# Convolution, windowed attention and a contractive recurrence on one core: QKV as a stage of its own, the image with its borders in DRAM, evenly spaced recurrence streams with a sixth of W z on TensorE

## The chip, the cores and the metric

The kernel runs on one core of a Trainium2 chip. The metric is device time in microseconds (us), as the median of several runs. One execution was also recorded by the hardware profiler; all views of the profile are of that execution. Engine names: PE is TensorE (PEld its weight loads), DVE is VectorE, ACT is ScalarE, POOL is GpSimd, SP is SyncE, which issues most of the DMAs.

## What is computed

The input is 32 images of 128 channels and 64 x 64 pixels, all float32. Cut to what matters:

```python
x = x + conv3x3(groupnorm(x), sum_k coeff[b, k] * kernels[k])     # its own kernel for each image
t = tokens(x)                                                     # (32, 4096, 128)
u = layernorm(t)
att = windowed_attention(u @ w_down.T)       # width 16, 4 heads of 4, windows of 144, step 72
t = t + layernorm(u + sigmoid(gate) * (att @ w_up.T))             # times gamma, plus beta
z = layernorm(t) @ W.T                                            # batch norm over all images and tokens
y[s] = sigmoid(scale * z[s] + shift + y[s-1] @ V.T)               # 4096 steps
out = t + y
```

The batch norm needs the mean and variance of z over all images, so the recurrence can begin only when the last image is through the rest.

## The kernel before, in words

**The image stage** (function images, with its clock). Channels lie on the 128 partitions and the 4096 pixels of an image on the free axis. The work on one image b is cut into Python generators:

- load(b) fetches the image into one of two frames xs of 66 x 66 (the image with a border of one pixel), takes its group norm, and mixes the four kernels into wb on DVE, with eight loads kx from DRAM.
- conv(b) transforms strips of the frame (ut, on POOL and DVE), multiplies them by wb (48 products of 512 columns for one image, PE nm<-ut,wb) and adds the results to the frame on DVE (xs<-xs,nm).
- project(b) writes the frame's inside to x_d in DRAM by four DMAs of quarters, takes squares and means for the layer norm (PE nm<-xs,avg and nm<-place,avg), sends reciprocal deviations through DRAM (r_d) and gets them back spread over all partitions (place<-r_d), normalizes into zt, projects to width 16 (PE sc<-zt,wd), transposes (DVE gt), and makes queries, keys and values (PE sc<-gt,wqB, wkB and sc<-wvB). All this is one generator. Queries and keys have one buffer, so its last part waits until attend(b-1) is through.
- attend(b) does 14 sets of two half-steps each. A half-step is four score products (PE sc<-qe,ks), one exponential of 128 x 1152 (ACT ex<-sc), and eight weighted sums of the half-step before (PE av<-ex,VE); every second half-step has four more sums (av<-ext,VT) and every fourth has four more scores (sc<-qs,kt). The score tile sc fills four banks of PSUM and has one buffer, so the next scores wait for the exponential.
- divide(b, 0) and divide(b, 1) divide by the softmax sums: the sums go out by DMA (cd<-av), a reciprocal, back by DMA (av<-cd), are spread by PE (sc<-av,spr), and the result goes through the output projection (sc<-av,wc) into zt.
- tail(b) does the second and third layer norm, reading the image back from x_d (place<-x_d), writes the token stream to the output, multiplies by W (PE nm<-zt,fWc) and writes z to z_d.

Engines execute in the order in which instructions are written. That order comes from a planner at the end of images: each generator yields which engine it wants next and which tiles it needs; class Clock keeps estimated times of every engine, tile and DMA; the loop takes the step that can start first and, among those that can start when PE comes free, the one that stands first in a list sorted by a due time, b plus a constant of the stage. Convolutions sort last, so they fill what the others leave.

**The recurrence** (by_runs). V contracts, so the 4096 steps of an image are cut into 128 runs of 32, each warmed up by 20 steps of the run before; one step handles the 128 runs of two images at once (256 columns). The 16 groups of two images go through four streams, group g in stream g mod 4. One step is: PE product v<-yw,fVT, DVE v<-zr,scl,v (adds scale times z, read with a stride of 32 elements), ACT sigmoid into yw, and, in the 32 real steps, a POOL copy over z in place. After its 52 steps a group is added to the output by two accumulating DMAs that POOL issues, and only then may SP load group g+6 into the same one of six buffers zr. The streams take turns, one step each in a round; stream j begins 8 j rounds after stream 0.

The lines that matter in what follows: L173 is the line of the planner's wrapper, through which all instructions of the image stage go, so the rows of that stage are told apart by their tiles. L1597 loads z, L1617, L1620, L1621, L1622 are the warm-up steps, L1626, L1627, L1630, L1631 the real steps, L1634 the output.

Of the kernel before, what the change touches and what calls it, by code (L numbers as in the profile page):

```python
# [8 lines left out]
F32 = mybir.dt.float32  # L9
# [31 lines left out]
class Clock:  # L41
# [79 lines left out]
    def cost(self, eng, op, out, ins):  # L121
        n = max(self.width(a) for a in (out, *ins))
        if eng == "PE":
            n = self.width(ins[1])
            k, m = int(ins[0].ap[0][1]), self.width(ins[0])
            full = k == P and m == P
            c = n / 600 + 0.04 if full else n / 2400 + (0.06 if m == P else 0.025)
            c += 0.09 * (full != self.full)
            self.full = full
            return c, c  # L130
        if eng == "SP":
            run = min(int(a.ap[-1][1]) for a in (out, *ins))
            return 0.8, 2.5 + (1.2e-5 if run >= 512 else 4e-5) * n * int(out.ap[0][1])
        if eng == "ACT":
            c = 0.17 + 0.00084 * n
        elif eng == "DVE":
            c = 0.18 + 0.00106 * n
            if op == "reciprocal":
                c = 0.1 + 0.0067 * n
        else:  # L140
            c = 0.5 + 0.0013 * n
        return c, c
# [46 lines left out]
def hybrid_kernel(  # L189
# [35 lines left out]
    r_d = dram.tile([NB, 3, 2, T], F32, name="r_d")  # L225
    x_d = dram.tile([NB, P, T], F32, name="x_d")
    z_d = dram.tile([NB, P, T], F32, name="z_d")
# [108 lines left out]


    QT, NPL, NF, NZ = T // 4, 5, 2, 3

    def images(nc):  # L340
# [6 lines left out]
        with ExitStack() as pa:  # L347

            frm = pa.enter_context(tc.tile_pool(name="frm", bufs=1))
            xs = [frm.tile([P, H + 2, W + 2], F32, name=f"xs{i}") for i in range(NF)]  # L350

# [171 lines left out]

            places = [kept([P, 4, UNIT], f"place{i}") for i in range(NPL)]
            spare = list(places)

            def spread(jobs):

                todo, got = list(jobs), []
                while todo or got:  # L530
                    if todo and len(got) < 3 and spare:
                        yield "SP", None, (todo[0][0],), (spare[0],)
                        if spare:
                            w = spare.pop(0).rearrange("p r t -> p (r t)")
                            nc.sync.dma_start(w, todo[0][0])
                            got.append((w, *todo.pop(0)))
                    elif got:
                        w, _, aps, use = got[0]
                        yield "DVE", None, (w,) + aps
                        use(w)  # L540
                        got.pop(0)
                        spare.append(w.rearrange("p (r t) -> p r t", r=4))
                    else:
                        yield

            def place(eng, aps):
# [6 lines left out]
                return spare.pop(0)  # L553

            def deviations(src, b, k, mean):

                dims = "p (c r y) w -> p r c y w" if k == 0 else "p (c r t) -> p r c t"
                parts = src.rearrange(dims, c=4, r=4)
                for r in range(4):
                    sq = yield from place("ACT", (src,))  # L560
                    nc.scalar.activation(
# [15 lines left out]
                    for c in range(4):  # L577
# [6 lines left out]
                        )  # L584
                    spare.append(sq)
                rs = yield from place("ACT", (ps,))
                var = ps[:, 0:UNIT]
# [12 lines left out]
                for c in range(4):  # L600
# [3 lines left out]
                    )  # L604
                spare.append(rs)

# [139 lines left out]
            def project(b):  # L746
# [4 lines left out]
                yield "SP", None, (rows(xt, 0, H),)  # L751
                for i in range(4):
                    nc.sync.dma_start(lines(x_d[b, :, quarter(i)]), rows(xt, 16 * i, 16))
                yield from deviations(rows(xt, 0, H), b, 0, True)
                while (b and ("proj", b - 1) not in done) or (b >= NZ and ("tail", b - NZ) not in done):
                    yield
# [3 lines left out]
                def normed(i, k):  # L760
                    z = zt[:, quarter(i)]
                    src = r_d[b, 0, 1 - k, quarter(i)].partition_broadcast(P)
                    if k == 0:
                        xi = rows(xt, 16 * i, 16)
                        return src, (xi,), lambda w: nc.vector.tensor_mul(lines(z), xi, lines(w))
                    return src, (z,), lambda w: nc.vector.tensor_sub(z, z, w)

                yield from spread(normed(i, k) for i in range(4) for k in range(2))
                done["frame", b] = True
                yield "PE", "sc", (zt[:, 0:T],)  # L770

# [35 lines left out]
                )  # L807
                while b and ("sets", b - 1) not in done:
                    yield
                yield "PE", "sc", (gt,)  # L810
                qs = one.tile([P, GT], F32, name="qs")
# [236 lines left out]
            def tail(b):  # L1048
# [5 lines left out]
                def second(i, k):  # L1054
                    z = zt[:, quarter(i)]
                    if k == 0:
                        return (
                            r_d[b, 1, 1, quarter(i)].partition_broadcast(P),
                            (z,),
                            lambda w: nc.vector.scalar_tensor_tensor(z, z, gam, w, ALU.mult, ALU.mult),  # L1060
                        )
                    return (
                        x_d[b, :, quarter(i)],
                        (z,),
                        lambda w: nc.vector.scalar_tensor_tensor(z, z, bet, w, ALU.add, ALU.add),
                    )
# [10 lines left out]
                def third(i):  # L1077
                    z = zt[:, quarter(i)]

                    def use(w):  # L1080
                        nc.vector.tensor_mul(z, z, w)
                        for j in range(2):
                            nc.vector.bn_stats(st[:, 2 * i + j, :], z[:, BLK * j : BLK * (j + 1)])

                    return r_d[b, 2, 1, quarter(i)].partition_broadcast(P), (z,), use
# [22 lines left out]
            for b in range(NB):  # L1108
                for stage, g in enumerate(
                    (tail(b), divide(b, 0), divide(b, 1), attend(b), project(b), load(b), conv(b))  # L1110
                ):
                    jobs.append([stage == 6, b + (0.4, -0.3, -0.3, 0.45, -0.65, -2.2, 0)[stage], b, g, None])
            while jobs:
# [17 lines left out]
    def images_by_shift():  # L1131

        with ExitStack() as pa:
            keep = pa.enter_context(tc.tile_pool(name="keep", bufs=1))
            NG5 = NH * (HD + 1)
            kT = keep.tile([P, NK, 9, P], F32, name="kT")
            nc.sync.dma_start(kT, conv_k.rearrange("m k i j l -> m k (i j) l"))

            avg = keep.tile([P, 2 * P], F32, name="avg")
            nc.vector.memset(avg, 0.0)  # L1140
            nc.vector.memset(avg[:, P : P + 1], 1.0 / P)

            row = keep.tile([P, NBLK, P], F32, name="row")
            nc.vector.tensor_copy(
# [71 lines left out]
            nc.gpsimd.memset(gx, 0.0)  # L1216
            mx = keep.tile([HALF, NWG, 2, P], F32, name="mx")
            nc.gpsimd.memset(mx, 0.0)
# [337 lines left out]
    with arm.Else():  # L1556
        images_by_shift()


# [20 lines left out]
    def by_runs():  # L1580
# [3 lines left out]
        with ExitStack() as pb:  # L1584
            zp = pb.enter_context(tc.tile_pool(name="zp", bufs=NSTR + 2))
            hp = pb.enter_context(tc.tile_pool(name="hp", bufs=1))
            p_v = pb.enter_context(tc.tile_pool(name="p_v", bufs=2, space=bass.MemoryType.PSUM))
            pb.enter_context(tc.manual_schedule())

# [3 lines left out]
            def load(g):  # L1593
                if g < NG:
                    zs[g] = zp.tile([P, NI, NRUN, RUN], F32, name="zr")
                    for i in range(NI):
                        nc.sync.dma_start(  # L1597
# [3 lines left out]
            for g in range(NSTR + 2):  # L1601
                load(g)

            def stream(j):
# [4 lines left out]
                for g in range(j, NG, NSTR):  # L1609
# [4 lines left out]
                    for r in range(RUN - WARM, RUN):  # L1614
# [3 lines left out]
                        else:  # L1618
                            ps = p_v.tile([P, NI, NRUN], F32, name=f"v{j}")[:, :, 1:]
                            nc.tensor.matmul(ps, fVT, yw[1 - r % 2][:, :, 1:], start=True, stop=True)  # L1620
                            nc.vector.scalar_tensor_tensor(ps, z, scl, ps, ALU.mult, ALU.add)  # L1621
                            nc.scalar.activation(y, ps, AF.Sigmoid, bias=shf)  # L1622
                        yield
                    for r in range(RUN):
                        ps = p_v.tile([P, NI, NRUN], F32, name=f"v{j}")
                        nc.tensor.matmul(ps, fVT, yw[1 - r % 2], start=True, stop=True)  # L1626
                        nc.vector.scalar_tensor_tensor(  # L1627
                            ps, zt[:, :, :, r], scl, ps, ALU.mult, ALU.add
                        )
                        nc.scalar.activation(yw[r % 2], ps, AF.Sigmoid, bias=shf)  # L1630
# [12 lines left out]
            step = 0  # L1643
            lag = 8
            while live:
# [117 lines left out]
```

## Time and profile before

| | us |
|---|---|
| median of three runs (lowest, highest) | 5713.89 (5710.51, 5716.48) |
| the profiled execution | 5711.31 |
| its span, first to last instruction | 5709.5 |
| PE busy | 4745.7 |
| DVE busy | 3681.2 |
| ACT busy | 2390.4 |
| POOL busy | 1594.0 |
| first exponential of attention, last one starts | 227.3, 4983.0 |
| last instruction on z, first on the recurrence's statistics | 5064.4, 5068.5 |
| first step of the recurrence | 5082.9 |
| last PE product | about 5676 |
| granted PE clock, mean | 0.925 |

A row of the profile's groups gives line, engine, operation, tiles (out<-in), shapes, the number of instructions, then busy time and mean length in ns, then the idle time of the engine just before them and what ended it. A float32 product shows as two PE records. A row of the stage windows gives the stretch, its length, busy time of PE, PEld, DVE, ACT and POOL with the number of instructions, the granted PE clock, the DMA engines' share and GB/s.

### The profile page before, as it was taken

How to read it: one execution, taken by the hardware profiler on the slowest of the kernel's cores; microseconds unless marked ns; L12 is line 12 of the kernel's file. 1: busy time of each engine (PE TensorE's matmuls, PEld its weight loads, DVE VectorE, ACT ScalarE, POOL GpSimd, SP SyncE). 2: the span in 40 equal slices, each digit the busy share in tenths (PEclk: the TensorE clock that was granted, in tenths of full speed). 3: DMA queues.
4: the chain of work that ended last, by engine and by line, in shares of the span. 5: the costliest groups of instructions: out<-in, count | busy, mean ns of one | idle time of the engine just before them, and what ended most of it. 6: DMA issues, size and time to landing. Idle time of an engine off the chain costs nothing. (4 is left out here: it accounts for less than half of the span.)

```text
span 5709.5 us, 105290 instructions
## 1 busy us (share of the span) xinstructions
PE 4745.7 (83%) x43443; PEld 2330.2 (41%) x43443; DVE 3681.2 (64%) x5175; ACT 2390.4 (42%) x3564; POOL 1594.0 (28%) x1561
## 2 busy tenths in 40 slices
PE   2898988898898897988898888888889887648886
PEld 1444434444444443444444444444444444314443
DVE  4656666666676666666666666666666665348886
ACT  0243434334444444444444434434444444326664
POOL 1232213122322222222232222322232221105555
PEclk9999999999899899999999999999989989869987
DMA  4535454545454445454644445454544444265887
GB/s 106 142 98 156 139 173 117 176 130 157 132 157 138 148 134 169 128 158 135 197 130 146 141 145 164 139 155 143 167 148 149 140 147 139 77 251 148 237 238 144
DMA packets 716380, 861.92 MB, mean 151 GB/s; under 512 B 560992, under 2 KB 571504, under 8 KB 687216
## 3 DMA queue, kind: packets, MB, share of 16 engines
q1 hardware_dynamic: 707184, 787.93, 44.4%
q0 software_dynamic: 8704, 67.11, 5.7%
q8 instruction: 347, 5.69, 0.4%
q14 instruction: 145, 1.19, 0.1%
HBM read 573.00 MB, written 273.68 MB: 148 GB/s over the span
## 5 line engine op out<-in xcount | busy, mean ns | idle before, releaser
L173 ACT ACTIVATE ex<-sc 128x1152 f32<-128x1152 f32 x896 | 1012.0, 1129 | 1344.6 <-PE sc L173 1334.3
L173 PE MATMUL nm<-ut,wb 128*128 128x512 f32 x3072 | 1540.1, 628 | 19.2 <-DVE wb L173 13.0
L173 PE MATMUL sc<-qe,ks 32*128 32x288 f32 x7168 | 731.1, 478 | 332.9 <-ACT ext L173 123.2
L173 POOL TENSOR_TENSOR qe<-qs,mqk 128x576 f32<-128x576 f32 x448 | 607.2, 1360 | 1412.2 <-PE sc L173 1358.9
L173 POOL TENSOR_TENSOR ut<-xs 128x576 f32<-128x576 f32 x384 | 549.7, 1461 | 1002.7 <-PE nm L173 784.6
L173 PEld LDWEIGHTS nm<-ut,wb 128*128 128x128 f32 x3072 | 540.3, 193 | 641.7 <-issue 610.7
L173 PE MATMUL av<-ex,VE 128*32 128x144 f32 x14336 | 659.7, 304 | 70.8 <-DVE av L173 70.4
L173 PEld LDWEIGHTS sc<-qe,ks 32*128 32x128 f32 x7168 | 301.8, 193 | 830.2 <-issue 280.5
L173 DVE TENSOR_TENSOR xs<-xs,nm 128x512 f32<-128x512 f32 (+1 forms) x640 | 494.4, 791 | 220.4 <-PE nm L173 208.0
L173 PEld LDWEIGHTS av<-ex,VE 128*32 128x32 f32 x14336 | 374.5, 113 | 411.3 <-issue 259.1
L173 DVE TENSOR_TENSOR zt<-zt,place 128x1024 f32<-128x1024 f32 x256 | 340.0, 1328 | 132.8 <-DMA place<-r_d 97.4
L1631 POOL COPY zr<-yw 128x256 f32<-128x256 f32 x512 | 302.9, 702 | 381.4 <-ACT yw L1630 220.4
L173 ACT ACTIVATE place<-zt 128x1024 f32<-128x1024 f32 x256 | 263.1, 1052 | 207.6 <-DVE zt L173 202.0
L1626 PE MATMUL v<-yw,fVT 128*128 128x256 f32 x1024 | 320.1, 439 | 22.6 <-ACT yw L1630 22.1
L173 DVE SCALAR_TENSOR_TENSOR wb<-kx,co,wb 128x768 f32<-128x768 f32 x192 | 254.0, 1323 | 113.9 <-DMA kx<-k_d 111.9
L1627 DVE SCALAR_TENSOR_TENSOR v<-zr,scl,v 128x256 f32<-128x256 f32 x512 | 308.2, 682 | 28.5 <-PE v L1626 27.1
L173 DVE TENSOR_TENSOR place<-place 128x256 f32<-128x256 f32 x416 | 204.4, 492 | 181.3 <-ACT place L173 172.0
L1620 PE MATMUL v<-yw,fVT 128*128 128x254 f32 x608 | 205.5, 448 | 118.1 <-ACT yw L1617 102.7
L173 PE MATMUL nm<-place,avg 128*32 128x256 f32 x3072 | 238.8, 401 | 54.2 <-ACT place L173 54.0
L173 PE MATMUL nm<-zt,fWc 128*128 128x512 f32 x512 | 262.9, 652 | 17.7 <-DVE xs L173 13.1
L1630 ACT ACTIVATE yw<-v,shf 128x256 f32<-128x256 f32 x512 | 241.6, 473 | 82.0 <-DVE v L1627 41.2
L173 DVE SCALAR_TENSOR_TENSOR zt<-sc,gbc,zt 128x576 f32<-128x576 f32 (+1 forms) x192 | 175.4, 913 | 149.4 <-PE sc L173 149.0
(186 smaller groups left out, 5519.4 us busy)
## 6 DMA issues: line engine op xcount, KB each, us to landing
place<-r_d SPq DMA_DIRECT2D x512, 512.0 KB
kx<-k_d SPq DMA_DIRECT2D x256, 384.0 KB
xs<-in_x_dram SPq DMA_DIRECT2D x128, 512.0 KB
x_d<-xs SPq DMA_DIRECT2D x128, 512.0 KB
place<-x_d SPq DMA_DIRECT2D x128, 512.0 KB
out_dram<-zt SPq DMA_DIRECT2D x64, 1024.0 KB
z_d<-zt SPq DMA_DIRECT2D x64, 1024.0 KB
zr<-z_d SPq DMA_DIRECT2D x32, 2048.0 KB
```

The lines of the kernel that those rows point to most:

```text
L173: got = f(*args, **kw)
L1620: nc.tensor.matmul(ps, fVT, yw[1 - r % 2][:, :, 1:], start=True, stop=True)
L1626: nc.tensor.matmul(ps, fVT, yw[1 - r % 2], start=True, stop=True)
L1627: nc.vector.scalar_tensor_tensor(ps, zt[:, :, :, r], scl, ps, ALU.mult, ALU.add)
L1630: nc.scalar.activation(yw[r % 2], ps, AF.Sigmoid, bias=shf)
L1631: nc.gpsimd.tensor_copy(zt[:, :, :, r], yw[r % 2])
```

## The change

1. project(b) ends after the transpose (it leaves the tiles in done["gt", b]); a new generator feed(b) makes queries, keys and values. The next image's zt may be taken when ("gt", b-1) is done instead of ("proj", b-1). The due times of all stages change, and the planner's price of a DMA changes (0.6 instead of 0.8 us of SP, and the cheap rate from rows of 128 elements on, not 512).
2. The two frames become one constant tile, frames, that outlives the image stage. x_d has rows of 66 pixels, so the image goes out with its side borders by one DMA of 128 contiguous pieces (four DMAs of rows of 64 pixels before); place tiles grow from 1024 to 1056 elements, and the tail reads the inside of a bordered strip.
3. When the last image has left its frame, the z of group 0 is loaded into the frames, and groups 0, 6 and 12 of the recurrence use them; five buffers zr are left for the others.
4. Stream j begins 13 j rounds after stream 0 (52 / 4) instead of 8 j.
5. In the steps with (r + j) divisible by 6, PE multiplies z by a diagonal matrix of the scale (dg) and adds V y to it in PSUM, in place of DVE's instruction: 132 of the 816 steps.

```diff
-            return 0.8, 2.5 + (1.2e-5 if run >= 512 else 4e-5) * n * int(out.ap[0][1])
+            return 0.6, 2.5 + (1.2e-5 if run >= 128 else 4e-5) * n * int(out.ap[0][1])
...
-    x_d = dram.tile([NB, P, T], F32, name="x_d")
+    x_d = dram.tile([NB, P, H, W + 2], F32, name="x_d")
...
+    frames = const.tile([P, NI, (H + 2) * (W + 2)], F32, name="frames")
+    framed = frames[:, :, 0:T]
...
-                for i in range(4):
-                    nc.sync.dma_start(lines(x_d[b, :, quarter(i)]), rows(xt, 16 * i, 16))
+                nc.sync.dma_start(x_d[b], xt[:, 1 : H + 1])
                 yield from deviations(rows(xt, 0, H), b, 0, True)
-                while (b and ("proj", b - 1) not in done) or (b >= NZ and ("tail", b - NZ) not in done):
+                while (b and ("gt", b - 1) not in done) or (b >= NZ and ("tail", b - NZ) not in done):
                     yield
...
                 done["frame", b] = True
+                if b == NB - 1:
+
+                    yield "SP", None, ()
+                    for i in range(NI):
+                        nc.sync.dma_start(framed[:, i], z_d[i])
+                while b and ("proj", b - 1) not in done:
+                    yield
                 yield "PE", "sc", (zt[:, 0:T],)
...
-                while b and ("sets", b - 1) not in done:
+                done["gt", b] = zt, gt, gf, gtt
+
+            def feed(b):
+
+                while ("gt", b) not in done or (b and ("sets", b - 1) not in done):
                     yield
+                zt, gt, gf, gtt = done["gt", b]
                 yield "PE", "sc", (gt,)
...
-                    (tail(b), divide(b, 0), divide(b, 1), attend(b), project(b), load(b), conv(b))
+                    (tail(b), divide(b, 0), divide(b, 1), attend(b), project(b), load(b), conv(b), feed(b))
                 ):
-                    jobs.append([stage == 6, b + (0.4, -0.3, -0.3, 0.45, -0.65, -2.2, 0)[stage], b, g, None])
+                    jobs.append([stage == 6, b + (-0.05, -0.15, -0.15, 1.65, -1.4, -2.8, 0, -1.2)[stage], b, g, None])
...
-            zp = pb.enter_context(tc.tile_pool(name="zp", bufs=NSTR + 2))
+            zp = pb.enter_context(tc.tile_pool(name="zp", bufs=NSTR + 1))
...
+            dg = hp.tile([P, P], F32, name="dgs")
+            nc.vector.tensor_scalar_mul(dg, ident, scl)
...
+                    if g % (NSTR + 2):
+                        zs[g] = zp.tile([P, NI, NRUN, RUN], F32, name="zr")
+                    else:
+                        zs[g] = framed.rearrange("p i (c r) -> p i c r", r=RUN)
+                    for i in range(NI if g else 0):
...
+            def product(ps, z, y, n):
+
+                if n % 6:
+                    nc.tensor.matmul(ps, fVT, y, start=True, stop=True)
+                    nc.vector.scalar_tensor_tensor(ps, z, scl, ps, ALU.mult, ALU.add)
+                else:
+                    nc.tensor.matmul(ps, dg, z, start=True, stop=False)
+                    nc.tensor.matmul(ps, fVT, y, start=False, stop=True)
...
-            lag = 8
+            lag = (WARM + RUN) // NSTR
```

The second arm of the image stage (images_by_shift), which does not run here, takes some of its constants from the frames as well; nothing of it is in the profile.

## The prediction

> **What bounds the kernel now.** I read the page's totals first, then rows of three stages, then each stage's waits. The profiled execution took 5711.3 us, 2.6 below the median of the runs shown; its span is 5709.5.
>
> ```profile
> PE 4745.7 (83%) x43443; PEld 2330.2 (41%) x43443; DVE 3681.2 (64%) x5175; ACT 2390.4 (42%) x3564; POOL 1594.0 (28%) x1561
> ```
> ```profile
> 300.00:4790.00 4490.00, 3920.49 (x38829) 1901.84 (x38828) 2924.34 (x3844) 1841.90 (x2517) 1173.32 (x918) 0.94 0.48 146
> 4790.00:5083.00 293.00, 162.78 (x1844) 79.85 (x1836) 119.35 (x163) 102.16 (x140) 26.26 (x22) 0.76 0.35 127
> 5083.00:5710.00 627.00, 489.63 (x1632) 263.13 (x1632) 472.29 (x846) 395.79 (x833) 331.70 (x544) 0.86 0.76 207
> ```
>
> The rows are the steady image stage, its end (no convolution left, two attentions alone) and the recurrence. In the first, PE is busy 3920 of 4490 us and no other engine comes near: PE's order is the bound, and 570 us of PE idleness the most that a better order can win. PE's waits there:
>
> ```profile
> PE sc L173 <- ACT ext L173: 120.8, 90, 4.7
> PE av L173 <- DVE av L173: 69.2, 27, 7.2
> PE sc L173 <- ACT VE L173: 66.2, 99, 6.1
> PE sc L173 <- ACT ex L173: 53.3, 86, 4.1
> ...
> PE sc L173 <- DMA av<-cd: 34.2, 9, 8.6
> ```
>
> 240 us (120.8 + 66.2 + 53.3) are waits of scores for ACT: half-steps of attention with nothing else for PE to do. The rows of the groups that price them:
>
> ```profile
> L173 ACT ACTIVATE ex<-sc 128x1152 f32<-128x1152 f32 x896 | 1012.0, 1129 | 1344.6 <-PE sc L173 1334.3 <-PE av L173 7.1 <-ACT place L173 0.3
> L173 PE MATMUL nm<-ut,wb 128*128 128x512 f32 x3072 | 1540.1, 628 | 19.2 <-DVE wb L173 13.0 <-POOL ut L173 5.9 <-DVE xs L173 0.3
> ```
>
> In the recurrence the chain of waits leaves the engines and runs through DMAs. Three rows of it, then rows of 20 us:
>
> ```profile
> 5200.70 22.79 DMA out_dram<-zr
> 5223.98 24.53 DMA zr<-z_d
> 5253.59 24.87 DMA zr<-z_d
> ```
> ```profile
> 5180.00:5200.00 20.00, 19.57 (x70) 10.11 (x68) 19.81 (x38) 16.97 (x37) 19.48 (x36) 1.00 0.00 0
> ...
> 5240.00:5260.00 20.00, 10.51 (x31) 7.45 (x32) 8.26 (x14) 7.80 (x17) 3.02 (x5) 0.62 1.03 268
> ...
> 5660.00:5680.00 20.00, 8.54 (x14) 3.50 (x14) 4.54 (x7) 3.79 (x8) 6.77 (x11) 0.50 1.04 214
> ```
>
> At 5180 DVE is full, POOL nearly (all four streams copy) and the DMAs idle; at 5240 the DMAs are full and DVE at 8 of 20. The streams end their groups close together, so storing and loading fall in a heap. That comes three times (5220 to 5290, 5380 to 5430, 5520 to 5580).
>
> **Part 1: the order of the image stage.** No computation is added or removed (feed is the last part of project). What changes shows in the order of the two built programs. Of the 895 stretches from one half-step's scores to the next's, 285 have nothing for PE beside attention before, 187 after; convolution products in stretches with at most three of them and no other large work are 452 before, 567 after. Timing those stretches by the 896 exponentials in the trace of before: empty 2.49 us, with one product 2.89; with extra scores 2.85 empty, 3.62 with two. So a product inside attention costs 0.39 us; on average it holds PE for 1.00 (1540.1 / 1536). 115 moved x 0.61 = 70 us. By medians (2.16 and 2.62) and the 0.858 us at which such products follow each other unhindered it is 115 x 0.40 = 46.
>
> The stretches between two images' attentions: 19 of 31 hold the projection to width 16 and last 47.2 us on average, the other 12 last 15.6. By the busy time of the rows for what PE does in them, the long ones hold 39.5 us of PE work, 7.7 less than they last; the short ones have none over. After, 10 are long, 21 short, because project may run ahead of feed. Nine conversions at 8 us (7.7, plus 1.5 for the short ones' overlap, less 1.2 where the moved pieces stand) are 72; with unhindered PE rates it is 61. Together 107 to 142. A third count, class means of all 895 stretches times the new numbers, corrected for their contents, gives 120. I take **120**. Bounds: 40 (half the lower fill, little of the rest) and 220 (waits for ACT gone, and half of what the clock loses: 80 stretches of the clock record from 300 to 4790 stand at 0.5, 508 us in all).
>
> The end from 4790 stays: both programs have two attentions there with no product left.
>
> **Part 2: the bordered image.** x_d leaves by one DMA of long pieces; before, four of 8192 rows of 256 bytes in all, each holding SP's queue 1.95 us. The DMAs stand at 0.48 in this stage, so I count 0. Bounds: +10 (the strips read back are 3% longer), and -20 out of DVE's 218 us of waits for place (97.4 + 79.1 + 26.6 + 15.2). DVE's add reads the strip in rows of 64: zt<-xs,place does it in 1339 ns against 1328 unstrided, so nothing.
>
> **Part 3: the start of the recurrence.** Before, stream 0 waits until 5082.9 for z. Shift and scale are ready at 5070.5. With z in place it can begin at 5071: **-12**. The two early loads stand on SP's queue ahead of one av<-cd of divide and wait for the last frame: at most 10 us once, beside attention.
>
> **Part 4: streams 13 rounds apart.** A round of four streams takes 2.25 us (DVE's four instructions start 0.56 apart), a lone stream 2.45 cold (5085 to 5109) and 1.95 warm. Groups now end 13 rounds, 29.25 us, apart. The DMA need of one group is 4.19 MB stored at 214 GB/s (last row above), 19.6 us, plus 4.19 MB loaded at 430 GB/s (5080 to 5120), 9.75: 29.3 us, just what there is. A load ends some 36 us after its buffer's group did and is needed after 26 rounds, 58 us: 22 us spare. So the heaps go. Sum in rounds: 13 x 2.45 + 26 x 1.95 + 169 x 2.25 + 39 x 2.0 = 541, then the last store, 24 us: 565. Before: 5083 to 5709.5, 626.5. **-61**.
>
> **Part 5: a sixth of W z by PE.** 132 DVE instructions of 0.56 become 132 products with dg. No row shows one. Its cost: at least 0.43 us, the pitch of v<-yw,fVT where none waits; at most 1.12, if both its passes pay for the stride what ACT does:
>
> ```profile
> L1622 ACT ACTIVATE yw<-v,shf 128x254 f32<-128x254 f32 x304 | 142.8, 472 | 53.8 <-DVE v L1621 39.6
> ...
> L1617 ACT ACTIVATE yw<-zr,shf,scl 128x254 f32<-128x254 f32 x16 | 13.0, 814 | 63.7 <-DMA zr<-z_d 63.6
> ```
>
> L1617 reads z with the stride, 342 ns more. Where the products fall decides: with streams 13 rounds apart, (r + j) mod 6 is the same for two or three streams, so of six rounds three or four have none and stay at DVE's 2.25, while a round with two or three holds PE for 2.6 to 3.0 (4 x 0.43 + 2 or 3 x 0.43). Six rounds: 4 x 2.25 + 2 x 2.6 = 14.2 at worst of this kind, 13.1 if evenly spread, 13.5 before. I take **0**; ends: -25 (the DMAs allow no more: 22 us spare over ten loads is a round of 2.1 us, 169 x 0.15), and +91 (132 x 0.69, all on the path).
>
> [...]
>
> **Sum.** 5711.3 - 120 - 12 - 61 = 5518; against the median, 2.6 more: **5520**.
>
> **Rivals.**
> - More in the image stage: fewer waits also keep the clock up, and 220 us go: 5420. For: 80 half-clock stretches, most of them after 3.4 us in which PE stood for half of the time or more. Against: the last 290 us and every third boundary stay.
> - Less in the image stage: the new order follows a plan, and the waits move (to kx, or to the divide that now stands inside attention in 21 images). 40 us instead of 120: 5600. For: 120 us of DVE waits for kx in the list of waits, and behind a waiting wb stand, on DVE, the additions xs that free the three nm buffers of PE.
> - Streams evenly apart, but the DMAs don't keep up with both directions at once and the heaps stay in part: half of the 61 is lost, 5550.
> - **Slower**: PE's read of z. If a dg product takes over 1.9 us, 132 x (1.9 - 0.43) eats the 193 us won. For: the stride, and the bunching that puts them on the path. Against: ACT's row gives 1.12 at the most.
> - The change does not do what it says: z of group 0 could come late, 12 us.
>
> **Chances.** Forecast (5450 to 5570) 0.52; more 0.16; less in either stage 0.25; slower 0.05; no change, within 0.2% (about what a measurement here can tell), 0.02. Faster is 0.93 in all. The range takes in the ends but for the outer parts: 5410 (220 and 98, all the ends on the fast side, give 5396) to 5640 (40 won in the images, the +91 end half paid).
>
> **What would show it.** Right: PE idle between 300 and the last convolution under 500 us; empty half-steps still at 2.2 to 2.6 us; 10 long boundaries; three 50 us holes of the recurrence gone, DMA share steady near 0.9 there; no load wait at its start. Wrong: dg products over 1 us apart, DVE waits for kx well over 120, or a DMA heap in the recurrence.

## The result, and the profile after

The changed kernel takes 5617.2 us (median; 5611.0 to 5619.0) against 5715.2 for the kernel before on the same chip (5710.5 to 5722.2): a ratio of 0.983, 95% interval [0.981, 0.984]. That is 98 us won where 193 were forecast. The time lies inside the stated range (5410 to 5640), but 97 us above the forecast and outside its band (5450 to 5570): it is the case "less in either stage", which had a chance of 0.25. The profiled execution took 5616.1 us (span 5614.3) against 5711.3, so its 95 us are what has to be found:

| stretch, us | before | after | change | forecast |
|---|---|---|---|---|
| start to shift and scale ready | 5070.5 | 4985.0 | -85 | -120 |
| from there to the recurrence's first step | 13.7 | 2.4 | -11 | -12 |
| first step to the end of the span | 625.4 | 626.9 | +1.5 | -61 |

The first step is counted from its first sigmoid, at 5084.2 before. (The 5082.9 named ahead of the prediction is where ACT begins to load its table for it, which takes 1.28 us.)

First the busy line of the page, then the stages (columns: span, PE, PEld, DVE, ACT, POOL, each with instructions, granted clock, DMA share, GB/s):

```profile
PE 4826.9 (86%) x43707; PEld 2388.9 (43%) x43707; DVE 3636.3 (65%) x5044; ACT 2391.4 (43%) x3564; POOL 1606.5 (29%) x1561
```
```profile
300.00:4705.00 4405.00, 3932.49 (x38706) 1880.41 (x38702) 2932.60 (x3816) 1842.26 (x2507) 1172.14 (x912) 0.95 0.48 150
4705.00:4985.00 280.00, 161.85 (x1892) 79.51 (x1892) 124.73 (x166) 104.99 (x143) 28.61 (x23) 0.79 0.39 138
4987.00:5614.00 627.00, 551.14 (x1896) 340.86 (x1896) 403.13 (x714) 390.16 (x833) 337.61 (x544) 0.92 0.78 207
```

The same PE work (3920 and 3932 us) is done in 4405 us instead of 4490. In the last row PE is busier than before (551 us against 490) and DVE less (403 against 472): that is the dg products' trade. PE's waits in the image stage (total, times, longest):

```profile
PE sc L173 <- ACT ext L173: 80.7, 68, 1.8
PE sc L173 <- POOL qe L173: 62.0, 40, 3.5
PE sc L173 <- DMA av<-cd: 59.1, 17, 8.1
PE sc L173 <- ACT ex L173: 53.3, 66, 2.0
PE sc L173 <- ACT VE L173: 46.7, 49, 2.7
PE nm L173 <- DVE mv L173: 41.6, 9, 5.4
```

The 69 us for "DVE av" are gone (1.5 left) and those for ACT ext and VE smaller; the wait for mv (the mean of a fetched image) has gone from 7 to 42 us, that for av<-cd from 34 to 59. On DVE:

```profile
DVE wb L173 <- DMA kx<-k_d: 139.4, 108, 2.9
DVE st L173 <- DMA frames<-in_x_dram: 93.8, 70, 7.0
```

These were 110 and 21 (xs for frames): DVE now waits for fetched images, and PE behind it for mv.

In the recurrence the chain has left the DMAs. Its summary from 5100 to 5500, then two rows of 20 us, the same stretches as before:

```profile
by line: PE v L1635 60.7%; PE v L1638 21.9%; PE v L1639 11.0%; DVE v L1636 3.6%; ACT yw L1663 1.7%; issue 0.7%; ACT yw L1658 0.4%; ACTq L1663 0.1%
```
```profile
5180.00:5200.00 20.00, 19.89 (x76) 13.37 (x75) 15.37 (x28) 14.34 (x31) 11.57 (x20) 1.00 0.89 185
5240.00:5260.00 20.00, 19.94 (x75) 12.88 (x74) 16.28 (x30) 15.19 (x33) 11.55 (x19) 1.00 1.03 247
```

The hole at 5240 is gone and the DMAs are busy in both rows (0.89, 1.03). But where DVE was full (19.8 of 20), it now stands at 15 to 16 and PE at 19.9; L1638, the dg product, alone is 22% of the chain. The rows of the groups follow. ACT's two are as before (472 and 814 ns there); a dg product shows as two records, of 600 ns in the mean:

```profile
L1658 ACT ACTIVATE yw<-v,shf 128x254 f32<-128x254 f32 x304 | 143.5, 473 | 81.4 <-DVE v L1636 60.1 <-PE v L1639 12.0
L1638 PE MATMUL v<-zr,dgs 128*128 128x256 f32 (+1 forms) x212 | 108.4, 600 | 0.0
L1654 ACT ACTIVATE yw<-zr,shf,scl 128x254 f32<-128x254 f32 x13 | 10.6, 815 | 0.0
```

From a dg product's start to the next product's start the trace has 0.846 us in the median (132 of them; the 212 records of the row are the 106 that read a buffer zr, the other 26 read the frames).

**Theory and rival.** For the recurrence: (A) the even spacing paid as forecast, and the strided dg products took it back; against it (B) the spacing pays little, because the DMAs can't serve both directions at once. For the image stage: (W) the boundaries gained nothing because transfers behind SP's queue come late; against it (M) the order alone sets the time, each kind of stretch keeping its mean, and the waits are incidental.

### The profile page after: what moved, and what is told of

Read it like the earlier page. It is cut to its first block, busy times and chain, and to the rows that moved or that the text cites. A ratio compares the mean times of both kernels' runs of the same rounds, so it can differ in the third digit from the quotient of the medians.

```text
span 5614.3 us, 105560 instructions
## 1 busy us (share of the span) xinstructions
PE 4826.9 (86%) x43707; PEld 2388.9 (43%) x43707; DVE 3636.3 (65%) x5044; ACT 2391.4 (43%) x3564; POOL 1606.5 (29%) x1561
## 3 DMA queue, kind: packets, MB, share of 16 engines
q14 instruction: 142, 1.16, 0.1%
## 5 line engine op out<-in xcount | busy, mean ns | idle before, releaser
L173 PE MATMUL nm<-ut,wb 128*128 128x512 f32 x3072 | 1599.6, 641 | 13.6 <-DVE wb L173 13.3
L173 POOL TENSOR_TENSOR qe<-qs,mqk 128x576 f32<-128x576 f32 x448 | 626.8, 1405 | 1316.2 <-PE sc L173 1292.3
L173 POOL TENSOR_TENSOR ut<-frames 128x576 f32<-128x576 f32 x384 | 538.9, 1433 | 870.1 <-PE nm L173 840.9
L173 DVE TENSOR_TENSOR frames<-frames,nm 128x512 f32<-128x512 f32 (+1 forms) x640 | 494.6, 791 | 290.1 <-PE nm L173 282.9
L1635 PE MATMUL v<-yw,fVT 128*128 128x256 f32 (+1 forms) x1368 | 389.5, 417 | 73.3 <-ACT yw L1654 27.3
L1636 DVE SCALAR_TENSOR_TENSOR v<-zr,scl,v 128x256 f32<-128x256 f32 (+1 forms) x557 | 333.7, 654 | 138.3 <-PE v L1635 137.1
L1635 PEld LDWEIGHTS v<-yw,fVT 128*128 128x128 f32 x1368 | 234.2, 194 | 215.6 <-ACT yw L1663 96.8
L173 DVE TENSOR_TENSOR place<-place 128x256 f32<-128x256 f32 x416 | 229.6, 552 | 137.5 <-ACT place L173 128.1
L1664 POOL COPY zr<-yw 128x256 f32<-128x256 f32 x416 | 261.4, 694 | 159.9 <-ACT yw L1663 159.7
L173 ACT COPY zt<-nm 128x512 f32<-128x512 f32 x256 | 150.1, 587 | 267.8 <-PE nm L173 267.7
```

What stands on the lines that cost most here:

```text
L173: got = f(*args, **kw)
L1635: nc.tensor.matmul(ps, fVT, y, start=True, stop=True)
L1664: nc.gpsimd.tensor_copy(zt[:, :, :, r], yw[r % 2])
```

## Experiments on the recurrence

Besides the time, each row gives the profiled recurrence, from its first step to the end of the span. Ratios are to the kernel before on the same chip. r1_no_dg and the seven kernels of the next section have the same recurrence to the instruction; it took 581.7 to 592.7 us in them, so a difference of some 10 us between two profiles says nothing.

| run | median us | ratio [95%] | recurrence us |
|---|---|---|---|
| changed kernel | 5617.2 | 0.983 [0.981, 0.984] | 626.9 |
| r1_no_dg | 5573.9 | 0.976 [0.973, 0.978] | 584.0 |
| r2_no_dg_lag8 | 5614.0 | 0.983 [0.981, 0.985] | 628.2 |
| r3_dg_lag8 | 5630.2 | 0.986 [0.984, 0.989] | 654.7 |
| r5_dg_contig | 5560.1 | 0.973 [0.970, 0.976] | 579.3 |
| r4_dg_spread | 5589.3 | 0.980 [0.978, 0.982] | 620.8 |

**r1_no_dg**: every step's W z on DVE.

```diff
-                if n % 6:
+                if n >= 0:
```

> The changed kernel with all 816 steps' W z on DVE again (no product with the diagonal matrix), streams 13 rounds apart. Theory A: the spacing is worth what was forecast, 61 us, and the 132 products with the strided z (0.85 us each in the trace of after, twice the 0.43 of the contiguous y) take it away again, by making TensorE the bound of the recurrence. Then a round is DVE's 2.25 us, the recurrence takes 565 us from its first step to the end instead of 627, and the kernel 5555 us. Theory B: the evenly spaced streams are bound by the DMAs or by their 247 rounds and win nothing whichever engine adds W z. Then 5610 to 5620.

The recurrence falls by 43 us, to 584.0, 19 more than theory A had it (565), and the kernel to 5573.9 (5555). A row of this kernel:

```profile
5180.00:5200.00 20.00, 20.00 (x72) 10.56 (x72) 20.00 (x37) 16.87 (x36) 13.86 (x24) 1.00 1.03 244
```

DVE does 37 instructions in 20 us, where the changed kernel's row had 28, with the DMAs full (1.03): they do keep up.

**r2_no_dg_lag8**: the same, with the streams 8 rounds apart again.

```diff
-            lag = (WARM + RUN) // NSTR
+            lag = 8
```

> The changed kernel with the recurrence's streams 8 rounds apart and all of W z on DVE, as before; only the early load of group 0 is left of the changes there. Theory A: the three holes of about 50 us with the DMAs full come back, the recurrence takes 625 us, as before, and the kernel 5615 us, 60 more than with 13 rounds and no product. Theory B: the same time as with 13 rounds.

628.2 us, near the 625.4 of before, and the holes are back:

```profile
5280.00:5300.00 20.00, 8.76 (x32) 4.46 (x30) 9.81 (x20) 7.20 (x16) 7.06 (x10) 0.79 1.02 310
```

So the spacing alone is worth 44 us (35.5 to 46.5 against the eight profiles of that recurrence), and B falls.

**r3_dg_lag8**: the dg products, the streams 8 apart (only the lag edit).

> The changed kernel with streams 8 rounds apart, products with the diagonal matrix kept. At 8 rounds the steps that take one do not fall in the same round. Theory A: the holes come back, and the rounds between them are at most as long as before, so 5600 to 5640. Theory B (spacing wins nothing): 5617, the same as after.

654.7: the products cost 26.5 us here and 43 with the even spacing. Part of their price may be hidden where the streams wait for DMAs anyway; at 8 rounds two streams' products also never fall in one round, and no run takes the two apart.

**r5_dg_contig**: the 132 products stay, but read a constant tile without a stride; those steps get a constant in place of W z.

```diff
+            flat = hp.tile([P, NI, NRUN], F32, name="flat")
...
-                    nc.tensor.matmul(ps, dg, z, start=True, stop=False)
+                    nc.tensor.matmul(ps, dg, flat[:, :, NRUN - y.shape[-1] :], start=True, stop=False)
```

> The changed kernel, but the 132 products with the diagonal matrix read a constant contiguous tile instead of z with its stride of 32 elements; so 132 steps get a constant in place of W z, and nothing else changes. Theory A: a product then takes 0.43 us instead of 0.85, 132 x 0.42 = 55 us less of TensorE's time, and the kernel takes 5560 to 5575 us. Rival: it is the second product's place in TensorE's queue that costs, not the stride; then the product still takes 0.8 us and the time stays at 5617.

579.3 us, 5 under r1_no_dg, which is no difference here. The next product follows after 0.431 us instead of 0.846. One product by itself, in the changed kernel and here (ns: least, median, most):

```profile
L1638 PE MATMUL v<-zr,dgs x212: 585/606/634, 5029.6 to 5575.4; 128*128 128x256 f32 x67, 128*128 128x254 f32 x39
```
```profile
L1640 PE MATMUL v<-flat,dgs x264: 377/379/635, 4993.2 to 5520.0; 128*128 128x256 f32 x84, 128*128 128x254 f32 x48
```

The same operation, the same weights, the same 132 products (264 records here; in the changed kernel 52 more on the frames, with a median of 607 ns): the price is in the operand that is read, and the added product as such costs nothing that can be told. The constant differs from z in its tile and its values too; that it is the stride is inferred, since no run reads z's own values without it.

**r4_dg_spread**: the strided products, but never two streams' in one round.

```diff
-                        product(ps, zt[:, :, :, r], yw[1 - r % 2], r + j)
+                        product(ps, zt[:, :, :, r], yw[1 - r % 2], turn[0] + (0, 1, 3, 4)[j])
...
+                turn[0] = step
```

> The changed kernel with its dg products (5617 us), but each round of the four streams has at most one stream, never two or three, whose step takes its W z from PE. A strided product holds PE for 0.85 us, so a round with one costs 4 x 0.43 + 0.85 = 2.57 us of PE, one with none 1.72. If bunching is what makes them cost 43 us (a round with two or three holds PE 3.4 to 4.3, the others wait for DVE at 2.25): mean round 4/6 x 2.57 + 2/6 x 2.25 = 2.46 against 2.53 now and 2.27 without dg, so 12 us back: about 5605. If the products simply add on PE, which is full in every round: no change, 5610 to 5625. If a single product hides beside DVE's work of its round: 40 us back, 5575 to 5585.

620.8 us, 6 less, with 135 products instead of 132 (a round counter places them). The bunching that the prediction worried about is at most a small part; the products add on PE wherever they stand. (The rest of this run's lead in the table lies in its image stage, whose order is that of the changed kernel: see the spread named under i10_plain_x.)

## Experiments on the image stage

All have r1_no_dg's recurrence, so r1_no_dg (5573.9) is their mark. "Stretches" is the sum of the 895 stretches between half-steps' scores; "boundaries" is how much longer the 31 stretches between two images last than the PE work in them, by the busy rates of PE's groups: a model. "PE idle" is how long PE stood idle in them by the trace. These three are of the one profiled execution, which was 8 us above the median in r1_no_dg, 17 above in i9_contig_fetch, 25 below in i8_old_order and 8 below in i1_old_price; six kernels with the changed kernel's image stage to the instruction (it and r1 to r5) have stretches of 4652 to 4680.

| run | median us | ratio [95%] | stretches us | boundaries us | PE idle us |
|---|---|---|---|---|---|
| before | 5715.2 | 1 | 4756 | 129 | 159 |
| changed kernel | 5617.2 | 0.983 [0.981, 0.984] | 4675 | 151 | 154 |
| r1_no_dg | 5573.9 | 0.976 [0.973, 0.978] | 4680 | 146 | 157 |
| i1_old_price | 5709.8 | 0.999 [0.998, 1.001] | 4795 | 147 | 139 |
| i2_piece_price | 5611.1 | 0.982 [0.979, 0.985] | 4696 | 66 | 135 |
| i3_old_due | 5671.6 | 0.993 [0.990, 0.995] | 4771 | 255 | 234 |
| i8_old_order | 5666.9 | 0.992 [0.989, 0.995] | 4743 | 110 | 150 |
| i9_contig_fetch | 5468.5 | 0.957 [0.955, 0.959] | 4578 | 66 | 98 |
| i10_plain_x | 5546.7 | 0.971 [0.970, 0.973] | 4655 | 143 | 149 |
| i12_pool_fetch | 5458.0 | 0.956 [0.954, 0.957] | 4544 | 21 | 70 |

**i1_old_price**: before's prices of a transfer in the planner.

```diff
-            return 0.6, 2.5 + (1.2e-5 if run >= 128 else 4e-5) * n * int(out.ap[0][1])
+            return 0.8, 2.5 + (1.2e-5 if run >= 512 else 4e-5) * n * int(out.ap[0][1])
```

> The changed kernel without dg products (that kernel took 5573.9 us), and with before's prices for a transfer in the planner: 0.8 us on SP's queue, and the slow landing rate for rows under 512 elements. Nothing else differs but the order that the planner then writes: 187 of the 895 stretches between two half-steps' scores hold one convolution product (295 with the new prices), 174 are empty (120), 1 boundary between two images holds the projection to width 16 (10). Theory M (the order alone decides, each kind of stretch keeps the mean that it has in the traces of before and after): the 895 stretches sum to 4612 to 4650 us against 4675, so 5510 to 5550 us in all: a boundary turned short is then worth something after all. Theory W (boundaries gain nothing, because every third one waits for fetched images and kx however the projection is placed): 54 more empty stretches cost about 0.6 us each, nothing comes back at the boundaries, about 4710 us of stretches and 5600 to 5610 us in all.

Both theories missed: 4795 us of stretches, 145 to 185 over M and 85 over W. Its PE waits tell where:

```profile
PE sc L173 <- DVE zt L173: 182.2, 59, 5.5
PE nm L173 <- DVE mv L173: 108.6, 26, 4.9
```

Against 34 and 42 in the changed kernel: each image's mean and normalized rows come late, and DVE itself waits 173 us for fetched images. The kinds of stretches say nothing of that.

**i2_piece_price**: SP's price by pieces, as measured.

```diff
-            return 0.6, 2.5 + (1.2e-5 if run >= 128 else 4e-5) * n * int(out.ap[0][1])
+            return 0.4 + 8e-4 * P * (n // run), 2.5 + (1.2e-5 if run >= 128 else 4e-5) * n * int(out.ap[0][1])
```

> The changed kernel without dg products (5573.9 us), with SP's price made to fit the trace: 0.4 us and 0.8 ns for each contiguous piece, so 2.0 us for a quarter image in rows of 256 bytes instead of 0.6. Theory W (the changed kernel's boundaries gain nothing because the planner thinks SP's queue free when it is held, so fetches, kx and av<-cd are late): PE's waits for av<-cd, DVE's for frames (94 us) and for kx (139 us) fall by half or more, and the time falls by 20 to 60 us to 5515 to 5555. Theory M (the order alone decides by its kinds of stretches; this one has 175 empty, 212 with one product, 16 long boundaries): 4729 to 4743 us of stretches against 4675, 5630 to 5640 us in all, whatever the waits do.

W's waits go as it said: PE's for av<-cd and mv fall from 59 and 42 to 1.7 and 5.8, DVE's for frames from 94 to 5, and the boundaries from 146 to 66 (PE's idle there only from 157 to 135: this order has 16 long ones); the wait for kx stays (139 to 125). The time does not follow, 5611 where W had 5515 to 5555: the new order has 55 more empty half-steps (without those that take extra scores), and other waits take the place:

```profile
PE sc L173 <- ACT ext L173: 104.3, 89, 2.3
PE sc L173 <- DVE zt L173: 98.7, 55, 6.0
```

Through the planner the question can't be asked cleanly, since a price rewrites the whole order.

**i3_old_due**: before's due times of the stages, the new prices.

```diff
-                    jobs.append([stage == 6, b + (-0.05, -0.15, -0.15, 1.65, -1.4, -2.8, 0, -1.2)[stage], b, g, None])
+                    jobs.append([stage == 6, b + (0.4, -0.3, -0.3, 0.45, -0.65, -2.2, 0, -0.65)[stage], b, g, None])
```

> The changed kernel without dg products (5573.9 us), with before's due times of the stages (feed at project's -0.65); the planner's new prices stay. Order: 180 empty stretches, 233 with one product, 16 long boundaries. If the due times made the gain of the image stage (85 us): back to about 4740 to 4755 us of stretches and 5640 to 5655 us in all. If the prices made it: no change, 5565 to 5585. By kinds of stretches with the means of before and after (theory M) 4700 to 4725, 5600 to 5625.

4771 us: the due times count, and more than M or its rivals had it; only with the next run does this get a meaning.

**i8_old_order**: before's due times and prices together.

> The changed kernel without dg products (5573.9 us), with before's due times and before's prices; the split of feed, the bordered image and the early load stay. The order that comes out is not before's: 292 empty stretches, 145 with one product, 28 long boundaries. Theory M: 4944 to 4949 us of stretches, so 5840 to 5850 us in all, 130 slower than before: due times and prices are worth more than the whole gain, and the bordered image or the split harms under the old ones. Theory S (the split and the bordered image help by themselves, whatever order is written): at or under before's image stage, 5640 to 5660 us in all.

With i1_old_price and r1_no_dg these make a square. By the medians: old prices and old due times 5667 us; the new prices alone 5672; the new due times alone 5710; both 5574 (stretches 4743, 4771, 4795, 4680). The new prices alone win nothing, the new due times alone lose 43 us, together they win 93: neither has a price of its own. M is refuted on both sides: i1_old_price is at least 145 us slower than it said, and i8_old_order, which has 292 empty half-steps (204 before by the same count) and was to sum to 4944 to 4949, is 200 us faster (some 175 with its median).

So the order has to be held still and the transfers changed.

**i9_contig_fetch**: the image lands as 4 KB pieces; the planner is told the old transfer, so that no engine's order changes.

```diff
-                    fetch(b)
+                    for i in range(4):
+                        at, src = (1 + 16 * i) * (W + 2) + 1, x[b, :, 16 * i : 16 * i + 16, :]
+                        nc.nc.sync.dma_start(frames[:, b % NF, at : at + QT], src.rearrange("p h w -> p (h w)"))
+                        nc.note("SP", "dma_start", (rows(gx, 16 * i, 16), src), {})
```

> The changed kernel without dg products (5573.9 us; its stretches between half-steps sum to 4680), every engine's order unchanged; only the image fetches land in SBUF as 4 KB pieces (128 to a quarter) instead of 256-byte rows (2048). The bordering of the fetched image is left out by this: its rows lie one after another, so the values are not the reference's, the amount of work is the same. An issue should then hold SP's queue some 0.4 us instead of 2.1. Theory W (the boundaries gained nothing because SP's queue is held by the fetches): PE's waits for av<-cd (59 us in the changed kernel) and for mv (42), and DVE's for frames (94) fall by more than half, the boundaries' time over PE's work falls from 150 us to about 70, and the time by 50 to 90 us, to 5485 to 5525. Rival: the fetches are late for another reason, or others wait behind them: waits move, time within 15 us of 5574.

102 us less in the stretches, 80 of them at the boundaries, and 5468.5 us, more won than W had. What it takes away is seen in the changed kernel's SP queue (start, us, instruction):

```profile
2397.95 7.05 SPq L173 DMA_DIRECT2D frames<-in_x_dram  x4
2405.05 4.54 SPq L173 DMA_DIRECT2D kx<-k_d  x2
2409.69 2.69 SPq L173 DMA_DIRECT2D av<-cd  x4
```

The reciprocals that av<-cd carries, and the product that needs them, in the same kernel:

```profile
2401.30 0.83 DVE L173 RECIPROCAL cd<-cd 128x108 f32<-128x108 f32 x1
2413.83 2.04 PE L173 MATMUL sc<-av,spr 24*32 24x432 f32 x7 [7.59 <-DMA av<-cd]
```

Four fetches and the kx behind them hold SP for 11.7 us, and av<-cd is issued at 2409.7, 7.6 us after its data are ready; PE stands idle for 7.6 us. Of the 64 such loads of the changed kernel 8 are issued more than 2 us late, 59 us in all; in this run none, 3 us in all. A fetch holds SP 2.27 us in the median there, 0.49 in this run (the hold seems to show on the issue after: the first of the four took 0.40 us, the others 2.0 to 2.3, the first kx 4.06, the second 0.43). PE's wait for av<-cd:

```profile
PE sc L173 <- DMA av<-cd: 26.4, 16, 3.2
```

from 59.1, and its longest from 8.1 to 3.2; the wait for mv falls from 42 to 11, DVE's for frames from 94 to 24. The wait for kx does not move (140).

**i12_pool_fetch**: the fetches as they were, in rows of 256 bytes, but from POOL's queue; orders unchanged otherwise.

```diff
-                    fetch(b)
+                    to, src = rows(gx, 16 * i, 16), x[b, :, 16 * i : 16 * i + 16, :]
+                    nc.nc.gpsimd.dma_start(to, src)
+                    nc.note("SP", "dma_start", (to, src), {})
```

> The changed kernel without dg products (5573.9 us), every engine's order unchanged but that the image fetches, still in rows of 256 bytes, are issued from POOL's queue instead of SP's. POOL is busy 26% in the image stage; its issues of the last stage, with 256 pieces each, hold it 1.45 us. If only SP's queue was the trouble (the run with contiguous fetches won 107 us), and a fetch holds POOL no longer than it held SP (2.1 us, 8.4 an image): 60 to 100 us won, 5475 to 5515. If issuing 2048 pieces holds POOL longer, qe and ut, which PE waits for, are late behind it: at 4 us an issue 30 images x 16 us, of which a third shows, 5575 to 5750. If the fetch is slow because of its pieces and not of the queue that issues them: frames come as late as before, 5555 to 5590.

5458.0 us, beyond the expected gain, with nothing of the computation left out: 136 us less in the stretches than r1_no_dg, 119 of them at the boundaries. DVE's wait for frames and PE's for av<-cd:

```profile
DVE st L173 <- DMA frames<-in_x_dram: 2.2, 3, 1.3
```
```profile
PE sc L173 <- DMA av<-cd: 17.7, 16, 2.6
```

The rows fetched are as short as before, though the profile counts POOL's fetches in another DMA queue (q0) with fewer packets: by the totals of the queues 144 a fetch there, 2064 on SP's. That it was not the fetch that was slow but SP's queue behind it is seen in the issue times: av<-cd is never issued late here (1.8 us in all), while a fetch that DVE waits for takes no less time from its issue to DVE's start (9.3 us in the median of 6 cases; 7.35 of 70 in the changed kernel). An issue holds POOL 1.16 us in the mean:

```profile
L639 POOL DMA_DIRECT2D frames<-in_x_dram x120 | 139.1, 1162 | 206.6 <-DVE zt L173 204.0 <-issue 2.5
```

The 204 us are POOL waiting, in its order, for the frame to come free; SP had stood idle just before its fetches for only 20 us in all in r1_no_dg. The 10 us between this run's median and i9_contig_fetch's lie within the spread of the latter (5446 to 5485).

SP's queue was not full in the changed kernel (its eight largest groups of issues sum to 1204 us of the 5614), only held at the wrong moments.

**i10_plain_x**: part 2 undone, the image to DRAM in four issues of 64-wide rows, orders unchanged.

```diff
-                nc.sync.dma_start(x_d[b], xt[:, 1 : H + 1])
+                for i in range(4):
+                    nc.nc.sync.dma_start(lines(x_u[b, :, quarter(i)]), rows(xt, 16 * i, 16))
+                nc.note("SP", "dma_start", (x_d[b], xt[:, 1 : H + 1]), {})
```

> The changed kernel without dg products (5573.9 us), every engine's order unchanged but that each image goes to DRAM by four issues in rows of 256 bytes, as before, not by one with its borders: part 2 undone. The prediction counted part 2 at 0, with bounds of -10 (this kernel 10 us faster) to +20. If SP's queue is what the image stage waits for (theory W), four issues of 2 us each and image more, 6 to 7 us of SP's time beside each conversion, cost 20 to 60 us here: 5595 to 5635. If SP has room for them: 5565 to 5595.

Faster than r1_no_dg by 0.4%, where W feared a loss. But runs whose image stage is the same to the instruction differ as much (4652 in r4_dg_spread, 4657 in r3_dg_lag8, 4680 in r1_no_dg), and this one's 4655 is among them: no effect is shown. So SP seems to have room where these stores stand, and to lack it where the fetches stand, ahead of av<-cd.

## Why the prediction was right or wrong

- **What bounds the kernel**: right in both stages. In the image stage the gain came out of PE's idle time (472 us of 4405 after, 570 of 4490 before). In the recurrence the three holes were the DMAs' (their share 1.03 in the row at 5240 before, and 1.02 in a hole of r2_no_dg_lag8).
- **Part 1, -120, measured -85** (its stretches -81; the same order in the other profiles -76 to -104). The fill paid a little more than its term (46 to 70): PE stood idle 233 us in the 285 empty half-steps before and 158 in the 187 after. The step that failed is "nine conversions at 8 us are 72". 10 long and 21 short boundaries came as foretold, but PE's idle in the 31 together only fell from 159 to 154 us. The step took the idle time for a property of the kind of boundary: that "the short ones have none over", and that a long one keeps what it had. Before, the 12 short ones held 1 us of idle; after, the 21 hold 52, of which 42 are waits for mv. The long ones went from 8.3 us each to 10.2, and in these 5.1 are waits for av<-cd, 0.7 before. Both waits are for transfers that SP's queue held up: with the fetches on POOL the same 31 boundaries, in the same order, have 70 us of idle, 90 less than before, so the step's 72 were there to be had. The prediction wrote down the hold (1.95 us an issue) and looked only at the stores it went away for, not at the fetches that stay. Its rival "less in the image stage" did name the divide, whose transfer av<-cd is; its sign "DVE waits for kx well over 120" came (139), but stays at 138 with the fetches on POOL, so it didn't point to what cost.
- **Its third count**, class means times new numbers, fails as a method: for four other orders it was off by 33 to 206 us, to both sides. That it was off by only 39 for the changed kernel (120 against 81) was luck.
- **Part 2, 0**: no effect is shown.
- **Part 3, -12, measured -11.**
- **Part 4, -61, measured -44** (r2_no_dg_lag8 less r1_no_dg). The mechanism was right. The mis-sized term is the ramps: r1_no_dg's rounds take 557.7 us against 541. Lone rounds and four-stream rounds are near (32.4 for the first 13, and 2.27 a round), but two- and three-stream rounds together, with the streams' last lone ones, take 141.6 instead of 128.7; the last store takes 26 instead of 24.
- **Part 5, 0, measured +43.** This is the other failed step. The range (-25 to +91) held it; the value taken was wrong. The rounds that gave it price a dg product at the lower end, 0.43 us, and ACT's 342 ns went into the upper end alone; 0.846 us lies in the middle between 0.43 and 1.12. Then "13.1 if evenly spread, 13.5 before" needed the product to hide in a PE that had 0.5 us free a round (2.25 less 4 x 0.43); r4_dg_spread shows that, evenly spread, it still costs 37 of the 43. With the contiguous operand the 0 would have been right (579.3 against 584.0). So the miss lies in the operand that PE reads: 0.846 us to the next product with the strided z, 0.431 with the constant.
- **The sum** fell between: -85 - 11 - 44 + 43, and 3 for the kernel's own lag-8 recurrence (628.2 in r2_no_dg_lag8, 625.4 before), make -94 of the profiled 95. Of the rivals, "less in the image stage" (waits move) and the price of dg each came half true.

Open: why new prices and new due times gain only together; and whether the kernel before would win as much from fetches on POOL's queue. Its trace shows the same thing, 11 of the 64 loads av<-cd issued more than 2 us late, but no run tried it.

## What to carry to other kernels

Give TensorE the operand that lies contiguous: here a product with the strided z took 0.846 us, and DVE's instruction on the same z 0.56. Price such a read by a run with a contiguous stand-in. Ask of a DMA issue how long it holds its queue and what stands behind it: a queue that is mostly idle can still be late just where PE waits (here 1204 us of issues in 5614, and 8 of the 64 loads av<-cd issued late, 59 us in all). And don't price a rewritten order by the mean of its stretches under the old one; hold the order still and change one transfer.

## What the runs showed of the hardware that was not expected

- A float32 product of 128x128 by 256 columns takes 0.431 us from start to next start with a contiguous moving operand, 0.846 with z at a stride of 128 bytes: 1.96 times.
- A fetch of a quarter image in 2048 rows of 256 bytes holds SP's queue 2.27 us in the median, one in 128 pieces of 4 KB 0.49; issued from POOL, the 2048 rows hold that engine 1.16 us.
